# Local attention stage: norms ahead of the last rotation, long sums ahead of the outputs, some multiplies by broadcast sums later, and half of the turned queries copied on ScalarE

## The chip, the cores and the metric

The kernel runs on one core of a Trainium2 chip. The metric is device time in microseconds (us) of one execution. Engines are called as the profile does: PE is TensorE (PEld its weight loads), DVE is VectorE, ACT is ScalarE, POOL is GpSimd, and SP is SyncE, which issues nearly all DMAs here. Each engine works through its own instructions in order; between engines, semaphores order what depends on what.

## What is computed

The input x is (4, 512, 256) in fp32, with a small vector (4, 64) beside it. Three residual parts follow one another: a mixture of experts (the best 2 of 8) with a linear attention, a full attention with gates and 16 heads, and a local stage. The change lies in the last one. Its two layers, cut to what matters:

```python
for l in range(2):
    q, k, v = split(shift_token(y) @ wqkv[l])      # 8 heads of 64 each
    q, k = l2norm(q) * q_scale, l2norm(k) * k_scale
    q, k = rotary_xpos(q, k)                       # q * cos * s + rotate_half(q) * sin * s
    o = local_attention(q, k, v)                   # windows of 128: a key's own and the one before
    y = y + merge(o) @ wo[l]
    u, g = split(layernorm(shift_token(y)) @ w1[l] + b1[l])    # 256 -> 2 x 682
    y = y + (u * gelu(g)) @ w2[l] + b2[l]
out = y + x                                        # all in fp32
```

`shift_token` takes the second half of the channels from the token before. `l2norm` divides a head's vector by its norm.

## The kernel before, in words

The span falls into the two earlier parts (0 to 695 us) and the local stage, `local_stream` (L607 on, 695 to 1339 us), which goes through two layers with four batches each. A batch is 512 tokens, four tiles of 128 (`NT`). All of y stays on chip.

For each layer and batch:
- `front` (L634): y is transposed on PE (`pdt`) and projected (`pdq`). For each tile t and for s = 0 (queries) and 1 (keys), ACT squares the projection (L658), DVE sums the squares per head (`ss`, L659), DVE multiplies the projection, read from PSUM, by a table of cosines (`t1`, L661) and its two exchanged halves by one of sines (`t2`, L665, two instructions), and POOL adds both to `qr` (L668). After all eight, ACT takes the root of all norms (L672, for which ACT loads a table of functions), DVE bounds it (L673) and inverts it (L674). ACT copies the values (L680). DVE multiplies a tile's queries by 1/norm (L686); PE transposes queries and keys (`pqt`), DVE copies the turned queries to `qT` and ACT the turned keys to `kT` (L693). The keys' 1/norm goes into the exponential as its scale.
- `scores` (L702) for each of four head pairs c: scores on PE (`pds`), exponentials on ACT (L720), masks on DVE (L723 128x384, L726 128x64).
- `values` (L747): products with v (`pn`), put together from two banks by an ACT copy (L744) and a DVE addition (L745) into `oT`; POOL adds parts of p (L753), from which `sums` (L755), called for every second c, forms the softmax's sums: a product with ones (`pz`), `z` (L744, L745), then a chain on the SP queue: z to DRAM and back as 128 rows (`rden`, L768, L769), reciprocal on DVE (L770), out again (`rows`, L772) and back as a broadcast to 64 partitions each (`zb`, L775). DVE multiplies two tiles of oT by zb (L778).
- `tail` (L780): product with wo (`pdy`), added to y by DVE (L784).
- `normed` (L789): y's shifted half by three DMAs into `hn`, statistics (L800 to L802), root (L804, L805), normalization (L808). `turned` (L810): hn transposed (`pht`), `hT` on DVE (L817), and then POOL's long sums: y += fb2 over all four tiles (L821, 128x1024), in layer 1 also y += x (L824). `hidden` (L826): gates and values (`pug`, `pua`), GELU on ACT (L835), products on DVE (L836). `output` (L855): second product (`pfy`), added to y by DVE (L871), in layer 1 with the DMA to the output.

PE's order is written by hand: everything below `PE.in_order()` is pinned to program order on PE (`keep_in_program_order`). The main loop runs over steps k = 4b + c, and interleaves generators:

```python
for k in range(4 * B + 2):
    if k > 1 and k % 2:  sums(l, b0, ds[b0], c0)     # of step k - 2
    if 0 < k <= 4 * B:   values(ds[b0], c0)          # of step k - 1
    if b < B:            scores(ds[b], c)
    spend(6 if b < B - 1 else 3)                     # pieces of the next front, of tail, of the feed-forward
```

So a batch's front runs beside the attention of the batch before, and `tail` of batch b - 1 beside that of b. `feed_forward` (L877) of batch 0 to 2 begins beside the attention of the last batch, b = 3; there `turned` for batch b + 1 comes ahead of `output` for batch b. The order on the other engines is chosen by a scheduler with its own estimates, within what data and pinned instructions allow. PSUM has eight banks in one ring for all these products, so a late reader holds up PE.

Of the kernel before, what the change touches and what calls it, by code (L numbers as in the profile page):

```python
# [67 lines left out]
def adaln_attn_ffn_kernel(ctx: ExitStack, tc: tile.TileContext, a: dict, out: bass.AP):  # L68
# [44 lines left out]
    def mmt(name):  # L113
        return bank("mm", name)
# [492 lines left out]
    def local_stream(dw, lp, y, dr):  # L607
# [23 lines left out]
            load(w.w1, a["f_w1"][l].rearrange("(c p) o -> p c o", p=128))  # L631
            load(w.w2, a["f_w2"][l].rearrange("(c p) o -> p c o", p=128))

        def front(w, b, d):  # L634

            yT = lp.tile([128, 2, S + 1], F32, tag="yT", name="yT", bufs=1)
            nc.gpsimd.memset(yT[:, 1, 0:1], 0.0)
            for c in range(2):
                pt = mmt("pdt")
                for k in range(NT):  # L640
                    PE.transpose(pt[:, k * 128 : (k + 1) * 128], y[b][:, k, c * 128 : (c + 1) * 128], ident)
                nc.scalar.copy(yT[:, c, 1 : S + 1], pt)
                yield

            def project(t, s):
                lhs = [yT[:, 0, 1 + t * 128 : 1 + (t + 1) * 128], yT[:, 1, t * 128 : (t + 1) * 128]]
                ps = mmt("pdq")
                mm(ps, [(lhs[c], w.wqkv[:, c, s * DIN : (s + 1) * DIN]) for c in range(2)])
                return ps.rearrange("p (h d) -> p h d", d=DHD)

            d.ss = ss = lp.tile([128, NT, 2, DH], F32, tag="ss", name="ss")
            qr = []
            for t in range(NT):
                qr_t = lp.tile([128, 2, DH, DHD], F32, tag="qr", name="qr", bufs=4)
                for s in range(2):
                    p3 = project(t, s)
                    sq = lp.tile([128, DH, DHD], F32, tag="tmp", name="sq", bufs=3)
                    nc.scalar.activation(sq, p3, AF.Square)  # L658
                    nc.vector.reduce_sum(ss[:, t, s, :], sq, axis=AX.X)  # L659
                    t1 = lp.tile([128, DH, DHD], F32, tag="t1", name="t1")  # L660
                    nc.vector.tensor_tensor(  # L661
                        t1, p3, w.tab[:, 2 * s, t, :].unsqueeze(1).to_broadcast([128, DH, DHD]), ALU.mult)
                    t2 = lp.tile([128, DH, DHD], F32, tag="tmp", name="t2", bufs=3)
                    for d0, d1 in ((0, 32), (32, 0)):
                        nc.vector.tensor_tensor(  # L665
                            t2[:, :, d0 : d0 + 32], p3[:, :, d1 : d1 + 32],
                            w.tab[:, 2 * s + 1, t, d0 : d0 + 32].unsqueeze(1).to_broadcast([128, DH, 32]), ALU.mult)
                    nc.gpsimd.tensor_tensor(qr_t[:, s], t1, t2, ALU.add)  # L668
                    yield
                qr.append(qr_t)  # L670

            nc.scalar.activation(ss, ss, AF.Sqrt)  # L672
            nc.vector.tensor_scalar_max(ss, ss, 1e-12)  # L673
            nc.vector.reciprocal(ss, ss)  # L674
            d.v = lp.tile([128, NT, DH, DHD], F32, tag="v", name="v")
            d.kT = lp.tile([128, 4, S], F32, tag="kT", name="kT")
            d.qT = lp.tile([128, 4, S], F32, tag="qT", name="qT")

            def value(t):
                nc.scalar.copy(d.v[:, t], project(t, 2))  # L680

            for t in range(3):
                value(t)
                yield
            for t in range(NT):
                nc.vector.tensor_tensor(  # L686
                    qr[t][:, 0], qr[t][:, 0], ss[:, t, 0].unsqueeze(2).to_broadcast([128, DH, DHD]), ALU.mult)
                for s, dst in enumerate((d.qT, d.kT)):
                    pt = mmt("pqt")
                    for c in range(4):  # L690
                        PE.transpose(pt[:, c * 128 : (c + 1) * 128],
                                     qr[t][:, s, 2 * c : 2 * c + 2, :].rearrange("p h d -> p (h d)"), ident)
                    (nc.vector.tensor_copy if s == 0 else nc.scalar.copy)(  # L693
                        dst[:, :, t * 128 : (t + 1) * 128], pt.rearrange("p (c q) -> p c q", q=128))
                    yield
                if t == 1:
                    value(3)
                    yield
# [53 lines left out]
                p = d.ps[c, r].rearrange("p (j q) -> p j q", q=192)  # L752
                nc.gpsimd.tensor_tensor(p[:, 1:, 0:64], p[:, 1:, 0:64], p[:, : NT - 1, 128:], ALU.add)  # L753

        def sums(l, b, d, c):  # L755
            z = lp.tile([128, S], F32, tag="z", name="z", bufs=1)
            pz = [mmt("pz") for g in range(2)]
            for i in range(4):
                ii = slice(32 * i, 32 * i + 32)
                p = d.ps[c - 1 + i // 2, i % 2].rearrange("p (j q) -> p j q", q=192)  # L760
                later = pz[1][ii].rearrange("p (j q) -> p j q", q=128)
                PE.matmul(pz[0][ii], ones32[0:64], p[0:64, :, 0:128], start=True, stop=True)
                PE.matmul(later[:, :, 64:], ones32[64:], p[64:, :, 0:64], start=True, stop=True)
                PE.matmul(later[:, 1:, 0:64], ones32[64:], p[64:, : NT - 1, 64:128], start=True, stop=True)
            together(z, pz)
            rd = rdenl[:, (l * B + b) * 2 + c // 2, :]
            sums_ = dr.tile([4, S], F32, tag="sums", name="sums")
            nc.sync.dma_start(sums_, z[0:128:32, :])  # L768
            nc.sync.dma_start(rd, sums_.rearrange("h q -> (h q)").rearrange("(p n) -> p n", p=128))  # L769
            nc.vector.reciprocal(rd, rd)  # L770
            rows_ = dr.tile([4, S], F32, tag="rows", name="rows")
            nc.sync.dma_start(rows_.rearrange("h q -> (h q)").rearrange("(p n) -> p n", p=128), rd)  # L772
            zb = lp.tile([128, 2, S], F32, tag="zb", name="zb", bufs=1)
            for r in range(2):
                nc.sync.dma_start(zb[64 * r : 64 * r + 64],  # L775
                                  rows_.rearrange("(c r) q -> r c q", r=2)[r].partition_broadcast(64))
            for i in range(2):
                nc.vector.tensor_tensor(d.oT[c - 1 + i], d.oT[c - 1 + i], zb[:, i, :], ALU.mult)  # L778

        def tail(w, b, d):  # L780
            for t in range(NT):
# [29 lines left out]
        def turned(l, b, f):  # L811
            f.hT = lp.tile([128, 2, S], F32, tag="hT", name="hT")
            for c in range(2):
                pt = mmt("pht")
                for k in range(NT):
                    PE.transpose(pt[:, k * 128 : (k + 1) * 128], f.hn[:, k, c * 128 : (c + 1) * 128], ident)
                nc.vector.tensor_scalar(f.hT[:, c, :], pt, col("lg", 2 * l + c), col("lb", 2 * l + c),  # L817
                                        ALU.mult, ALU.add)
                yield

            nc.gpsimd.tensor_tensor(  # L821
                y[b], y[b], row("fb2")[:, l * H : (l + 1) * H].unsqueeze(1).to_broadcast([128, NT, H]), ALU.add)
            if l == 1:
                nc.gpsimd.tensor_tensor(y[b], y[b], xres[b], ALU.add)  # L824

        def hidden(l, w, f):  # L826

# [49 lines left out]
        def feed_forward(l, w):  # L877
            fs = [SimpleNamespace() for b in range(B)]
            normed(0, fs[0])
            yield  # L880
            yield from turned(l, 0, fs[0])
            for b in range(B):
                for i, _ in enumerate(hidden(l, w, fs[b])):
                    yield b
                    if i == 0 and b + 1 < B:
                        normed(b + 1, fs[b + 1])
                if b + 1 < B:
                    yield from turned(l, b + 1, fs[b + 1])
                yield from output(l, w, b, fs[b])


# [7 lines left out]

        def first_two(w, ds):
            first, second = (front(w, b, ds[b]) for b in range(2))

            def lead():
                for _ in range(20):
# [5 lines left out]
                yield from first  # L912
            return lead(), [second] + [front(w, b, ds[b]) for b in range(2, B)]

        lead, second = first_two(wa, ds)
        run(lead)
        with PE.in_order():
            for l in range(2):
# [26 lines left out]
                def spend(n):  # L945
                    for _ in range(n):
                        next(fill, None)

                for k in range(4 * B + 2):
                    b, c = divmod(k, 4)  # L950
                    if k > 1 and k % 2:
                        b0, c0 = divmod(k - 2, 4)
                        sums(l, b0, ds[b0], c0)
                    if c == 0 and b < B:
                        run(fill)
                        fill = beside(b)
                    if 0 < k <= 4 * B:
                        b0, c0 = divmod(k - 1, 4)
                        values(ds[b0], c0)
                    if b < B:  # L960
                        scores(ds[b], c)
                    spend(6 if b < B - 1 else 3)
# [21 lines left out]
                nxt = iter(())  # L984
                if l == 0:
                    wa = attn_weights(1)
                    nxt, second = first_two(wa, ds)
                for at in ff:
                    if at is not None and at >= 2:
                        break  # L990
# [1124 lines left out]
```

## Time and profile before

| | |
|---|---|
| runs, us | 1336.31, 1340.78, 1344.16 |
| median, us | 1340.78 |
| profiled execution, us | 1341.16 |
| its span, us | 1339.4 |
| mean granted clock of PE | 0.983 |
| POOL busy, us | 292.8 (22%) |
| DMA, mean over the span | 64 GB/s |

The span is the stretch from the first to the last instruction of the profiled execution; its own time is 1.8 us longer. In timeline lines of the profile the first two numbers are the start and the duration in us, then come engine, line, operation, output<-input by the program's names, shape, and in brackets the idle time of the engine before it with what ended that; "x2" stands for two like instructions in a row, and the duration is then of both. A line of waits gives the waiting group, what released it, the sum, the number of times and the longest. The granted clock is the share of PE's full clock that it was allowed.

### The profile page before, as it was taken

Reading aid. Unit: us, or ns where it says so; the run is one execution under the profiler, and the core shown is the slowest. Engines: PE = TensorE matmul, PEld = TensorE weight load, DVE = VectorE, ACT = ScalarE, POOL = GpSimd, SP = SyncE. Lnnn points to the kernel's source line nnn. Section 1 sums busy time; section 2 is a strip of 40 time slices with the busy share of each in tenths; the row PEclk is TensorE's granted clock in tenths of the full one; section 3 lists DMA queues with packets and bytes.
Section 4 is the critical chain, followed back from the end, with each engine's and each line's share of the span. In section 5 each row is a group of like instructions: output and inputs, shape, how many; then the busy total and the mean of one; then the engine's idle time right before and its main releaser. Section 6 shows DMA issues by size and latency. Waiting matters only on the chain.

```text
span 1339.4 us, 23071 instructions
## 1 busy us (share of the span) xinstructions
PE 1273.7 (95%) x9214; PEld 812.9 (61%) x9214; DVE 685.6 (51%) x1464; ACT 581.6 (43%) x1158; POOL 292.8 (22%) x321
## 2 busy tenths in 40 slices
PE   4899999998999999999999999999999998999998
PEld 3788899964566634444344655766556556667654
DVE  6221243425777734241247798654362877864421
ACT  3221233226655365656644646561222655464111
POOL 1322356420000201010103334210030333422010
PEclk7999999998999999999999999999999999999999
DMA  3565666523000000000220001311001011012000
GB/s 95 212 232 199 233 235 226 183 101 101 0 1 1 1 1 1 0 1 1 91 71 1 18 18 27 104 34 25 24 0 44 25 30 31 18 43 57 17 20 23
DMA packets 41856, 85.29 MB, mean 64 GB/s; under 512 B 9409, under 2 KB 25673, under 8 KB 39433
## 3 DMA queue, kind: packets, MB, share of 16 engines
q1 hardware_dynamic: 36600, 73.02, 16.9%
q0 software_dynamic: 3504, 9.46, 2.1%
q8 instruction: 77, 1.26, 0.4%
q10 hardware_dynamic: 1632, 1.21, 0.3%
q14 instruction: 43, 0.34, 0.1%
HBM read 74.76 MB, written 6.82 MB: 61 GB/s over the span
## 4 chain that ended last, share of the span: by engine, by line
PE 76%; DVE 10%; DMA 6%; ACT 4%; issue 3%; POOL 0%; SPq 0%; DVEq 0%; POOLq 0%
PE ph L82 11%; PE pdq L82 7%; PE pfy L82 6%; PE sc L82 6%; PE pua L82 5%; PE pug L82 5%; PE pv L82 5%; PE pdy L82 4%; PE po L82 3%; PE pn L82 3%; DMA ys<-ob,goal 2%; PE pds L82 2%; PE pqk L82 2%; PE pz L82 1%; PE pqt L86 1%
## 5 line engine op out<-in xcount | busy, mean ns | idle before, releaser
L82 PE MATMUL pdq<-wqkv,yT 128*128 128x512 f32 x384 | 172.4, 599 | 2.5 <-DVE t L665 2.2
L424 ACT ACTIVATE cex<-sc 128x512 f32<-128x512 f32 x256 | 132.0, 605 | 85.8 <-PE sc L82 84.8
L82 PEld LDWEIGHTS pdq<-wqkv,yT 128*128 128x128 f32 x384 | 71.5, 191 | 85.0 <-issue 76.7
L82 PE MATMUL ph<-h,w 128*128 128x256 f32 (+2 forms) x576 | 121.4, 369 | 0.3 <-ACT h L1635 0.3
L668 POOL TENSOR_TENSOR qr<-t,t 128x512 f32<-128x512 f32 x64 | 81.3, 1271 | 138.2 <-DVE t L665 138.2
L82 PEld LDWEIGHTS ph<-h,w 128*128 128x128 f32 x576 | 101.5, 191 | 15.7 <-ACT h L1635 0.5
L1500 DVE TENSOR_SCALAR h<-ph,w 128x256 f32<-128x256 f32 (+2 forms) x52 | 23.0, 462 | 122.1 <-PE ph L82 101.6
L82 PE MATMUL sc<-qm,kT 32*128 32x512 f32 x512 | 83.0, 647 | 0.0
L720 ACT ACTIVATE p<-pds,ss 128x192 f32<-128x192 f32 (+1 forms) x256 | 79.8, 425 | 2.1 <-PE pds L82 0.8
L82 PE MATMUL pua<-hT,w 128*128 128x512 f32 x160 | 75.3, 593 | 1.1 <-DVE z L745 1.1
L82 PE MATMUL pug<-hT,w 128*128 128x512 f32 x160 | 76.1, 598 | 0.0
L658 ACT ACTIVATE sq<-pdq 128x512 f32<-128x512 f32 x64 | 38.5, 601 | 84.0 <-POOL qr L668 46.6
L753 POOL TENSOR_TENSOR p<-p 128x192 f32<-128x192 f32 x64 | 42.1, 678 | 137.7 <-PE pn L82 134.9
L835 ACT ACTIVATE gl<-pug,cols 128x512 f32<-128x512 f32 x40 | 27.3, 687 | 93.3 <-PE pug L82 90.4
L82 PE MATMUL pv<-cex,v 128*32 128x512 f32 x512 | 61.7, 598 | 2.7 <-DVE vw L378 2.7
L82 PE MATMUL pfy<-w,uA 128*128 128x256 f32 x256 | 61.4, 383 | 0.0
L82 PE MATMUL po<-w,h 128*128 128x256 f32 x264 | 60.1, 380 | 0.0
L723 DVE TENSOR_TENSOR p<-p,lmask 128x384 f32<-128x384 f32 x64 | 47.1, 736 | 23.2 <-ACT p L720 21.8
L82 PE MATMUL pdy<-wo,oT 128*128 128x256 f32 x256 | 58.7, 383 | 0.0
L1498 ACT ACTIVATE h<-ph,w 128x256 f32<-128x256 f32 (+2 forms) x52 | 22.4, 455 | 82.5 <-PE ph L82 78.7
L82 PE MATMUL pn<-p,v 64*64 64x128 f32 (+1 forms) x1792 | 50.4, 254 | 7.6 <-DVE p L726 3.7
L836 DVE SCALAR_TENSOR_TENSOR uA<-pua,cols,gl 128x512 f32<-128x512 f32 x32 | 23.8, 749 | 65.6 <-PE pua L82 56.1
(361 smaller groups left out, 2325.1 us busy)
## 6 DMA issues: line engine op xcount, KB each, us to landing
w<-in_moe_w_dram SPq DMA_DIRECT2D x18, 1024.0 KB, 8.3
w<-in_moe_w_dram SPq DMA_DIRECT2D x18, 516.0 KB, 3.8
w<-in_moe_w_dram SPq DMA_DIRECT2D x14, 640.0 KB, 4.3
zb<-rows SPq DMA_DIRECT2D x32, 256.0 KB, 4.2
g<-ys SPq DMA_DIRECT2D x6, 512.0 KB, 6.4
wqkv<-in_f_wqkv_dram SPq DMA_DIRECT2D x2, 1536.0 KB
w<-in_f_w_dram SPq DMA_DIRECT2D x2, 1408.0 KB
w<-in_moe_w_dram SPq DMA_DIRECT2D x4, 512.0 KB
```

The lines of the kernel that those rows point to most:

```text
L82: cls._queue(nc.tensor.matmul(*args, **kw))
L86: cls._queue(nc.tensor.transpose(*args, **kw))
L424: nc.scalar.activation(ex[:, i, :], pss[2 * j + i], AF.Exp, scale=CHD**-0.5)
L658: nc.scalar.activation(sq, p3, AF.Square)
L668: nc.gpsimd.tensor_tensor(qr_t[:, s], t1, t2, ALU.add)
L720: nc.scalar.activation(p[:, j * 192 : j * 192 + n], pss[j // 2][r][:, j % 2 * 192 : j % 2 * 192 + n], AF.Exp, scale=d.ss[:, j, 1, 2 * c + ...
L723: nc.vector.tensor_tensor(edges, edges, lmask[:, :128].rearrange("p (s q) -> p s q", q=64).unsqueeze(1).to_broadcast([128, 3, 2, 64]), ALU ...
L753: nc.gpsimd.tensor_tensor(p[:, 1:, 0:64], p[:, 1:, 0:64], p[:, : NT - 1, 128:], ALU.add)
L835: nc.scalar.activation(gl, pg, AF.Gelu, bias=col("bg", l * (NU + 1) + i))
L836: nc.vector.scalar_tensor_tensor(f.u[i // 4][:, i % 4, :], pa, col("ba", l * (NU + 1) + i), gl, ALU.add, ALU.mult)
L1498: pinned(nc.scalar.activation(dst, src, AF.Relu, bias=bias))
L1500: pinned(nc.vector.tensor_scalar(dst, src, bias, 0.0, ALU.add, ALU.max))
```

## The change

- In `front`, the root, the bound and the reciprocal stand after t1 of the last projection (t = 3, s = 1) and ahead of its t2, and so do the multiplies by 1/norm of the query tiles 0 and 1. DVE's instructions among these, and the last two halves of t2, are pinned to program order. Tiles 2 and 3 are multiplied where they were.
- In the very first front (`awake=4`), ACT takes a root of one element early, and PE makes four products of 128x128 into the bank of the first `pqt` ahead of its transposes.
- The turned queries of the tiles 1 and 3 are copied by ACT.
- POOL's long sums leave `turned(l, b)` for a new `residual(l, b)`, pinned, ahead of `output(l, b)`.
- The multiplies by zb become a function that `sums` returns. For c0 = 1 it is called one step later, after `values`, and pinned; for batch 2 and c0 = 3 two steps later, inside the next `sums` behind z, and pinned; for the others at once, as before.

PE's order is the same but for the four products, SP's is the same. In the built kernel the multiplies by zb stand elsewhere on DVE at three steps: for batch 1, c0 = 1, they come after the two additions of `oT` at k = 8; for batch 2, c0 = 3, after z at k = 15; for batch 3, c0 = 1, after the two additions of `oT` at k = 16. The sums of batch 0 and 1 on POOL stand right after the last additions of p (k = 16), with a clearing of `hn` behind each. Those of batch 2 and 3 stand, in layer 0, after the fifth and the eighth addition of `qr` of the next layer's first front, and in layer 1 after the last clearing of `hn`.

```diff
-        def front(w, b, d):
+        def front(w, b, d, awake=0):
...
             qr = []
+            if awake:
+                root = lp.tile([128, 1], F32, tag="rs", name="root")
+                nc.scalar.activation(root, eps5, AF.Sqrt)
+
+            def unit(t):
+                tc.keep_in_program_order(nc.vector.tensor_tensor(
+                    qr[t][:, 0], qr[t][:, 0], ss[:, t, 0].unsqueeze(2).to_broadcast([128, DH, DHD]), ALU.mult))
+
             for t in range(NT):
...
                         t1, p3, w.tab[:, 2 * s, t, :].unsqueeze(1).to_broadcast([128, DH, DHD]), ALU.mult)
+                    if t == NT - 1 and s == 1:
+                        nc.scalar.activation(ss, ss, AF.Sqrt)
+                        tc.keep_in_program_order(nc.vector.tensor_scalar_max(ss, ss, 1e-12))
+                        tc.keep_in_program_order(nc.vector.reciprocal(ss, ss))
+                        for t0 in range(2):
+                            unit(t0)
                     t2 = lp.tile([128, DH, DHD], F32, tag="tmp", name="t2", bufs=3)
                     for d0, d1 in ((0, 32), (32, 0)):
-                        nc.vector.tensor_tensor(
+                        ins = nc.vector.tensor_tensor(
                             t2[:, :, d0 : d0 + 32], p3[:, :, d1 : d1 + 32],
                             w.tab[:, 2 * s + 1, t, d0 : d0 + 32].unsqueeze(1).to_broadcast([128, DH, 32]), ALU.mult)
+                        if t == NT - 1 and s == 1:
+                            tc.keep_in_program_order(ins)
                     nc.gpsimd.tensor_tensor(qr_t[:, s], t1, t2, ALU.add)
...
-            nc.scalar.activation(ss, ss, AF.Sqrt)
-            nc.vector.tensor_scalar_max(ss, ss, 1e-12)
-            nc.vector.reciprocal(ss, ss)
             d.v = lp.tile([128, NT, DH, DHD], F32, tag="v", name="v")
...
             for t in range(NT):
-                nc.vector.tensor_tensor(
-                    qr[t][:, 0], qr[t][:, 0], ss[:, t, 0].unsqueeze(2).to_broadcast([128, DH, DHD]), ALU.mult)
+                if t > 1:
+                    nc.vector.tensor_tensor(
+                        qr[t][:, 0], qr[t][:, 0], ss[:, t, 0].unsqueeze(2).to_broadcast([128, DH, DHD]), ALU.mult)
                 for s, dst in enumerate((d.qT, d.kT)):
                     pt = mmt("pqt")
+                    if t + s == 0 and awake:
+                        with PE.in_order():
+                            for _ in range(awake):
+                                PE.matmul(pt[:, 0:128], ident, ident, start=True, stop=True)
                     for c in range(4):
...
                                      qr[t][:, s, 2 * c : 2 * c + 2, :].rearrange("p h d -> p (h d)"), ident)
-                    (nc.vector.tensor_copy if s == 0 else nc.scalar.copy)(
+                    (nc.vector.tensor_copy if s == 0 and t % 2 == 0 else nc.scalar.copy)(
                         dst[:, :, t * 128 : (t + 1) * 128], pt.rearrange("p (c q) -> p c q", q=128))
...
-        def sums(l, b, d, c):
+        def sums(l, b, d, c, before):
             z = lp.tile([128, S], F32, tag="z", name="z", bufs=1)
...
             together(z, pz)
+            if before is not None:
+                before(True)
             rd = rdenl[:, (l * B + b) * 2 + c // 2, :]
...
                                   rows_.rearrange("(c r) q -> r c q", r=2)[r].partition_broadcast(64))
-            for i in range(2):
-                nc.vector.tensor_tensor(d.oT[c - 1 + i], d.oT[c - 1 + i], zb[:, i, :], ALU.mult)
+
+            def scaled(pin):
+                for i in range(2):
+                    ins = nc.vector.tensor_tensor(d.oT[c - 1 + i], d.oT[c - 1 + i], zb[:, i, :], ALU.mult)
+                    if pin:
+                        tc.keep_in_program_order(ins)
+            return scaled
...
-            nc.gpsimd.tensor_tensor(
-                y[b], y[b], row("fb2")[:, l * H : (l + 1) * H].unsqueeze(1).to_broadcast([128, NT, H]), ALU.add)
+        def residual(l, b):
+            tc.keep_in_program_order(nc.gpsimd.tensor_tensor(
+                y[b], y[b], row("fb2")[:, l * H : (l + 1) * H].unsqueeze(1).to_broadcast([128, NT, H]), ALU.add))
             if l == 1:
-                nc.gpsimd.tensor_tensor(y[b], y[b], xres[b], ALU.add)
+                tc.keep_in_program_order(nc.gpsimd.tensor_tensor(y[b], y[b], xres[b], ALU.add))
...
                     yield from turned(l, b + 1, fs[b + 1])
+                residual(l, b)
                 yield from output(l, w, b, fs[b])
...
-        def first_two(w, ds):
-            first, second = (front(w, b, ds[b]) for b in range(2))
+        def first_two(w, ds, awake):
+            first, second = front(w, 0, ds[0], awake), front(w, 1, ds[1])
...
-        lead, second = first_two(wa, ds)
+        lead, second = first_two(wa, ds, 4)
         run(lead)
...
+                late = {}
                 for k in range(4 * B + 2):
...
                         b0, c0 = divmod(k - 2, 4)
-                        sums(l, b0, ds[b0], c0)
+                        scaled = sums(l, b0, ds[b0], c0, late.pop(k, None))
+                        due = k + (1 if c0 == 1 else 2 if b0 == B - 2 else 0)
+                        if due == k:
+                            scaled(False)
+                        else:
+                            late[due] = scaled
                     if c == 0 and b < B:
...
                         values(ds[b0], c0)
+                    if k in late:
+                        late.pop(k)(True)
                     if b < B:
...
                     wa = attn_weights(1)
-                    nxt, second = first_two(wa, ds)
+                    nxt, second = first_two(wa, ds, 0)
                 for at in ff:
...
                         break
```

## The prediction

> **What bounds the kernel now.** I read the page from the top: busy time, the slices, then the chain that ended last.
>
> ```profile
> PE 1273.7 (95%) x9214; PEld 812.9 (61%) x9214; DVE 685.6 (51%) x1464; ACT 581.6 (43%) x1158; POOL 292.8 (22%) x321
> ...
> PE 76%; DVE 10%; DMA 6%; ACT 4%; issue 3%; POOL 0%; SPq 0%; DVEq 0%; POOLq 0%
> ```
>
> TensorE (PE) is busy for 95% of the span. The change leaves its work alone (but for four 128x128 matmuls), so only PE's idle time and its clock can be won. Second come PE's waits in the local stage (690 to 1340 us), as releaser, sum, times, longest:
>
> ```profile
> PE pqt L86 <- DVE qr L686: 9.5, 7, 2.5
> PE pn L82 <- DVE p L726: 3.7, 2, 2.3
> PE pn L82 <- DVE p L723: 3.6, 4, 0.9
> PE pdq L82 <- DVE t L665: 2.2, 4, 0.7
> PE pds L82 <- DVE t L665: 2.2, 3, 1.0
> PE pua L82 <- DVE z L745: 1.1, 1, 1.1
> ```
>
> The reader sees that all of this is 23 us, and that VectorE (DVE) releases nearly all of it. Third, stretches of one clock step around two of the three largest gaps (PE, PEld, DVE, ACT, POOL busy, granted clock, DMA share, GB/s):
>
> ```profile
> 714.56:717.97 3.41, 0.89 (x8) 0.82 (x8) 2.74 (x5) 1.03 (x3) 1.11 (x1) 1.00 0.00 0
> 717.97:721.38 3.41, 3.41 (x13) 2.60 (x12) 2.16 (x4) 1.17 (x2) 0.00 (x0) 0.50 0.00 0
> 1127.57:1130.98 3.41, 1.06 (x30) 0.68 (x28) 3.41 (x3) 1.99 (x5) 3.19 (x3) 1.00 0.63 154
> 1130.98:1134.39 3.41, 3.41 (x62) 3.23 (x62) 3.24 (x5) 1.33 (x4) 1.74 (x2) 0.50 0.01 2
> ```
>
> After a stretch with over 2.3 us of idle PE the clock is 0.50 for 3.41 us, and so it is after the third, 1182.18 to 1185.59, with 2.38 idle. That costs half of it, 1.7 us, on top of the gap. The dips' starts lie whole multiples of 3.413 us apart (121 from the first to the second), so whether a gap near 2.3 us brings one depends on where it falls; I take one half.
>
> Last, the DVE's order around the gap at 1127.71, and POOL beside it:
>
> ```profile
> 1126.42 2.19 DVE L723 TENSOR_TENSOR p<-p,lmask 128x384 f32<-128x384 f32 x1 [0.45 <-ACT p L720]
> 1128.53 2.36 DVE L726 TENSOR_TENSOR p<-p,lmask 128x64 f32<-128x64 f32 x1
> ```
>
> ```profile
> 1125.19 3.00 POOL L821 TENSOR_TENSOR yc<-yc,drows 128x1024 f32<-128x1024 f32 x1 [3.49 <-DVE hn L808]
> 1128.13 0.10 POOL L637 MEMSET yT<- 128x1 f32 x1
> 1128.27 2.54 POOL L824 TENSOR_TENSOR yc<-yc,xres 128x1024 f32<-128x1024 f32 x1
> ```
>
> Undisturbed, the two masks take 0.56 and 0.22 us; beside a long sum they end with it. Instructions of DVE that read PSUM (0.68 and 0.41 us for L661 and L665) do not grow beside POOL. So two inputs from SBUF on DVE and a sum on POOL exclude each other, one whole instruction at a time. Beside this, the Trainium skill ("SBUF — State Buffer", section "Who interferes with whom") calls the pair's shared port an exclusive lock; the masks agree, and by it the moved multiplies of part F, for which there is no row, would be held just like them.
>
> **The change part by part**, against the profiled execution (1341.16 us, span 1339.4; the median of the runs is 1340.78). Negative is a gain.
>
> A, first front. PE waits 2.52 us at 714.66 for the unit queries (L686).
>
> ```profile
> 713.58 0.75 DVE L665 TENSOR_TENSOR t<-pdq,tab 128x256 f32<-128x256 f32 x2
> 715.16 0.56 DVE L673 TENSOR_SCALAR ss<-ss 128x64 f32<-128x64 f32 x1 [0.84 <-ACT ss L672]
> 715.76 0.55 DVE L674 RECIPROCAL ss<-ss 128x64 f32<-128x64 f32 x1
> 716.35 1.89 DVE L686 TENSOR_TENSOR qr<-qr,ss 128x512 f32<-128x512 f32 x3
> ```
>
> With the table loaded ahead (1.28 us) and two t2 halves (0.75) out of the way, the Sqrt runs at 713.6 behind a v copy of ACT, maximum 0.18, reciprocal 0.55 and the first multiply 0.68 end at 715.3, not 717.0: 1.7 us off the gap. What is left is about 0.75 us, so the dip goes too, 1.7 us. Late next is ACT, which gets two query copies (0.58 each, as its copies of kT) ahead of the exponentials: these start about 724.25 and not 727.07. **-2.8** (-1.1 if there had been no dip).
>
> The four matmuls stand in what is left of the gap, and cost nothing while it is over 1 us; else up to 4 x 0.16 us (a pqt transpose: 0.63 for four). Beside it, the Trainium skill ("TensorE: Matmul & The Clock Gate", "Part 1: The HAM clock gate") halves the clock after a wholly idle window of some 3.4 us; the window agrees with the 3.413 us here, but not the idle share, since 2.35 of 3.41 was enough. By that rule none of these gaps would bring a dip, and the change would be worth 3.4 us less.
>
> B, fronts of b=1, no sums near (749.05, 1.04 us; 1062.76, 1.04). The first multiply no longer stands behind the last halves (0.75) nor beside the last qr addition (0.5): PE 1.0 earlier, of which the next z keeps 0.25. **-0.75 twice**. In layer 1 the query copy of t=3 goes ahead of the first exponentials: 0.58 by its row, 0.27 after the slack there. **+0.3**.
>
> C, fronts of b=2 with sums in the masks. Layer 0: gaps 791.03 (1.14) and 813.06 (0.94) go. PE gains 1.9, but in the next stretch DVE is the later one (its reductions stand behind a multiply by zb that waits until 816.61 for its DMA): **-1.4** stays. Layer 1: 0.95 + 1.40 (the sums in the masks), 1.1 of the multiply gap 1105.65 (1.15) and the dip's 1.7 would make 5.15; the sums' removal leaves exponentials as next late, so **-4.4** (-3.5 for another place on the clock's steps).
>
> D, fronts of b=3 (840.19, 1.12; 1157.78, 1.52). DVE must now wait for the Sqrt, which has a v copy and a table load (1.28) ahead of it: 0.5 to 1.2 us of idle DVE with the last halves, a value copy and the multiply by zb queued behind it. **-0.9** and **-1.25**. The cover is thin: pdy needs oT at 844.95 and I find the multiply's end at 844.75.
>
> E, the multiplies said to be later. In the built order those before 870.91 and 1182.74 keep their place; z at 1172.94 to zb at 1183.05 is a chain of DMAs on SP that is not shortened. The gaps (1.10 and 2.27) stay. The dip at the second is a coin toss, -0.9 in the mean.
>
> F, long sums before outputs, b=3. This speaks against the change. For batches 0 and 1 the sums come to stand right behind POOL's last p additions, which end at 902.91, with nothing to wait for. Just there DVE gets its multiplies by zb:
>
> ```profile
> 903.56 1.29 DVE L778 TENSOR_TENSOR oT<-oT,zb 128x512 f32<-128x512 f32 x2 [2.53 <-DMA zb<-rows]
> 904.77 1.15 DVE L745 TENSOR_TENSOR oT<-pn,oT 128x448 f32<-128x448 f32 x2
> ...
> 907.80 0.61 DVE L745 TENSOR_TENSOR z<-pz,z 128x448 f32<-128x448 f32 x1
> ...
> 918.96 1.29 DVE L778 TENSOR_TENSOR oT<-oT,zb 128x512 f32<-128x512 f32 x2 [2.45 <-DMA zb<-rows]
> ```
>
> The two oT rows now come ahead of the multiplies. Sum 0 runs 902.95 to 905.33 (2.38, its row at 914.02), the first multiply to 905.9, sum 1 to 908.3, the second multiply to 908.9. Then y, two hT, statistics and z follow as in the trace: z ends 2.85 later than 908.41. From z to the last zb are 10.5 us of DMAs and a reciprocal behind statistics that slip too, so zb lands at 921.9, not 918.96; with the multiply (0.65) oT is ready at 922.55, where PE wants it for pdy at 920.2, and 0.25 goes for the fourth part of oT. **+2.6**. Layer 1 has two sums a batch: z 2.5 later, zb at 1241.85, oT at 1242.5, wanted at 1240.76, and 0.15 in the same way: **+1.9**. Bounds: 0 if the second multiply gets in between the sums (z then fits its slack of 0.55 and 0.83); +1.7 more if the first gap halves the clock, +0.85 in the mean.
>
> G. Sums 2 and 3 of layer 0 stand among the next layer's qr additions (1.27 each), where PE has no gaps: 0; if that cover fails, one sum, 2.4. Sixteen copies leave DVE (0.69 each) for ACT (0.58), 44% busy: 0 outside A and B.
>
> Sum: -2.8 - 0.75 - 1.4 - 0.9 + 2.6 + 0.3 - 0.75 - 4.4 - 1.25 + 1.9 = -7.45; the two mean dips (-0.9, +0.85) cancel. 1341.16 - 7.45 = 1333.7, **1334 us**.
>
> **The rivals.**
> R1, no collision in F: the second multiply gets in first. For: memsets stand between the sums. Against: a multiply already held while a sum runs, as the masks above. -7.45 - 4.5: 1329.
> R2, slower: the pinned queue on DVE decides. In six inner fronts the maximum waits up to 1.2 us for the Sqrt, and a held instruction 1.27 (a qr addition); halves and multiplies by zb queue behind, and PSUM's banks with them. It decides once the multiply by zb is later than pdy (0.2 us of slack, D). 6 x 2.47 = +14.8: 1348.5. For: D's thin slack. Against: at 748.06 the maximum follows without a wait.
> R3, no difference: the table loads and copies on ACT become the late ones in A and C, so -2.8, -1.4 and half of -4.4 go: 1340.
> R4, the dips stay, since other gaps bring them: -7.45 + 3.4: 1337. This is also what the page's rule on idle windows would give; three dips behind three largest gaps speak against it.
>
> **How the numbers follow.** Forecast 0.47 (own range 1331 to 1337), R1 0.20, R2 0.12, R3 0.13, R4 0.08. The range reaches from R1 with an end of its own (E's dip, 1.7) to R3 with the bounds of F and A: 1327 to 1343.5; R2 and thin tails stay out. A change under 0.5% (6.7 us, below 1334.1) cannot be told from none here: half of the forecast and all of R1 are faster, 0.44; the rest, R3 and R4 same, 0.44; R2 slower, 0.12.
>
> **What would show it.** A: pqt starts near 715.4 and no 0.50 clock follows. B, D: waits of pqt for L686 fall from 9.5 to about 3 us. C: masks of b=2 at 0.56 and 0.22. E: the gap at 1182.74 is still there. F: multiplies L778 near 903 stretched to over 1.5 us, and pdy waiting near 920. It is wrong if those stay 0.65 each, or if DVE idles for L672 while PE waits for pdy.

## The result and the profile after

The median goes from 1339.54 us (21 runs, 1335.57 to 1346.53) to 1335.37 us (21 runs, 1330.7 to 1339.1). The ratio is 0.9963, with a 95% interval of 0.9952 to 0.9975: 3 to 6 us faster. The forecast was 1334, from a sum of -7.45 us. The profiled executions differ by 5.9 us (1341.16 and 1335.27; spans 1339.4 and 1333.5), the medians by 4.2. The forecast subtracted its sum from the one profiled execution, which lies 1.6 us above the median of the 21; so the time of 1334 was met more closely (1.4 us) than the gain.

PE's waits in the local stage after (releaser, sum, times, longest). Lines have moved: L679 is t2, L658 the early unit multiply, L800 the multiply by zb, L741 and L744 the masks, L763 the additions into oT and z:

```profile
PE pdy L82 <- DVE oT L800: 4.0, 2, 2.4
PE pdq L82 <- DVE t L679: 3.2, 4, 0.9
PE pua L82 <- DVE z L763: 2.7, 1, 2.7
PE pn L82 <- DVE p L744: 2.2, 1, 2.2
PE pds L82 <- DVE t L679: 1.8, 3, 1.0
PE pn L82 <- DVE p L741: 1.7, 2, 0.8
PE pqt L86 <- DVE qr L658: 1.5, 4, 0.4
```

The first line of before, pqt for the unit queries with 9.5 us, is now the last with 1.5. A line that before did not have, pdy for oT with 4.0 us, heads the list. One wait has been exchanged for another.

To see where the time went, I took the start of the same PE instructions in both traces and followed their difference through the stage. Each step of it belongs to one part of the prediction:

| part, at (before's time) | forecast | measured |
|---|---|---|
| A, first front (717 to 722) | -2.8 | -3.5 |
| B, layer 0 (750) | -0.75 | -0.7 |
| C, layer 0 (792 to 831) | -1.4 | -1.4 |
| D, layer 0 (841) | -0.9 | -0.7 |
| E, layer 0 (871) | 0 | +1.65 |
| F, layer 0 (921) | +2.6 | +2.0 |
| B, layer 1 (1064 to 1070) | -0.45 | -0.5 |
| C, layer 1 (1107 to 1149) | -4.4 | -4.5 |
| D, layer 1 (1159) | -1.25 | -1.1 |
| E, layer 1 (1188) | 0 (mean of a dip -0.9) | -1.7 |
| F, layer 1 (1241) | +1.9 | +4.5 |

With +0.15 ahead of the stage and -0.2 of rests the measured column gives the -5.9, but for rounding. The two misses in E nearly cancel; both are luck, as is worked out below.

Stretches of one clock step after, with the columns as before (PE, PEld, DVE, ACT, POOL busy, granted clock, DMA share, GB/s). The first is the stretch that had 2.52 us of idle PE; the others lie around the second wait of pdy, in layer 1:

```profile
714.56:717.97 3.41, 3.41 (x27) 3.02 (x26) 3.38 (x7) 1.94 (x4) 1.20 (x1) 1.00 0.00 0
1230.12:1233.53 3.41, 1.03 (x5) 0.33 (x4) 1.35 (x3) 0.00 (x0) 0.00 (x0) 1.00 0.42 121
1233.53:1236.94 3.41, 3.41 (x6) 1.85 (x6) 1.32 (x3) 0.00 (x0) 0.00 (x0) 0.50 0.00 0
```

So the first front has neither gap nor half clock any more, and the new gap of 2.38 us has brought one. That is 1.7 of the 4.5 us of F in layer 1.

VectorE and POOL at the place of part F, layer 0, after:

```profile
898.39 1.16 DVE L763 TENSOR_TENSOR oT<-pn,oT 128x448 f32<-128x448 f32 x2 [1.86 <-ACT oT L762]
899.47 4.59 DVE L800 TENSOR_TENSOR oT<-oT,zb 128x512 f32<-128x512 f32 x2
903.98 0.41 DVE L809 TENSOR_TENSOR yc<-pdy,yc 128x256 f32<-128x256 f32 x1
```

```profile
898.37 2.37 POOL L847 TENSOR_TENSOR yc<-yc,drows 128x1024 f32<-128x1024 f32 x1
900.67 0.20 POOL L818 MEMSET hn<- 1x128 f32 x1
900.84 2.67 POOL L847 TENSOR_TENSOR yc<-yc,drows 128x1024 f32<-128x1024 f32 x1
```

The two multiplies took 1.29 us before and take 4.59 now: the first ends half a microsecond after sum 0 (900.74), the second after sum 1 (903.51). The masks of batch 2, layer 1, are undisturbed in return:

```profile
1121.50 0.55 DVE L741 TENSOR_TENSOR p<-p,lmask 128x384 f32<-128x384 f32 x1
1121.97 0.22 DVE L744 TENSOR_TENSOR p<-p,lmask 128x64 f32<-128x64 f32 x1
1122.64 0.56 DVE L741 TENSOR_TENSOR p<-p,lmask 128x384 f32<-128x384 f32 x1 [0.46 <-ACT p L738]
```

### The profile page after: what moved, and what is told of

Read it like the earlier page. It is cut to its first block, busy times and chain, and to the rows that moved or that the text cites. A ratio compares the mean times of both kernels' runs of the same rounds, so it can differ in the third digit from the quotient of the medians.

```text
span 1333.5 us, 23089 instructions
## 1 busy us (share of the span) xinstructions
PE 1273.4 (95%) x9222; PEld 809.9 (61%) x9222; DVE 672.4 (50%) x1448; ACT 588.7 (44%) x1175; POOL 294.6 (22%) x321
## 3 DMA queue, kind: packets, MB, share of 16 engines
q10 hardware_dynamic: 1632, 1.21, 0.3%
## 4 chain that ended last, share of the span: by engine, by line
PE 72%; DVE 9%; DMA 9%; ACT 6%; issue 3%; POOL 1%; SPq 0%; POOLq 0%; DVEq 0%
PE ph L82 11%; PE pdq L82 7%; PE sc L82 6%; PE pv L82 5%; PE pug L82 5%; PE pua L82 5%; PE pfy L82 5%; PE pdy L82 4%; PE po L82 3%; PE pn L82 3%; DMA zb<-rows 2%; DMA ys<-ob,goal 2%; PE pqk L82 2%; PE pds L82 1%; PE pf L82 1%
## 5 line engine op out<-in xcount | busy, mean ns | idle before, releaser
L82 PEld LDWEIGHTS pdy<-wo,oT 128*128 128x128 f32 x256 | 47.9, 191 | 16.2 <-DVE oT L800 5.7
L82 PEld LDWEIGHTS pua<-hT,w 128*128 128x128 f32 x160 | 30.3, 190 | 41.5 <-issue 35.8
```

What stands on the lines that cost most here:

```text
L82: cls._queue(nc.tensor.matmul(*args, **kw))
```

## The experiments

The theory was that the norms' move is the gain, and that moving the sums gives back in F about what it wins in C. The rival was that the sums' move is itself the gain and pdy's new wait comes from something else. Ratios are to the kernel before, run on the same chip. The changed kernel's own ratio is 0.9963 [0.9952, 0.9975].

**Hold the sums behind the multiplies.**

```diff
         def residual(l, b):
+            if b < 2:
+                gate = lp.tile([1, 1], F32, tag="gate", name="gate", bufs=1)
+                tc.keep_in_program_order(nc.gpsimd.tensor_copy(
+                    gate, y[0][0:1, 0, 0:1] if b else ds[B - 1].oT[1][0:1, 0:1]))
```

> The changed kernel, with the long sums of batches 0 and 1 held back by a copy of one element: for batch 0 it reads oT of the last batch behind its multiplies by zb, for batch 1 it reads y of batch 0 behind its outputs. The order on every other engine is that of the changed kernel. Theory (the sums exclude the multiplies, and what follows on VectorE is late for pdy): the pair of multiplies takes 1.3 us and not 4.59, the two waits of pdy (1.61 and 2.38 us) and the half clock behind the second (1.7 us) go, and the time falls by 4 to 5 us, to about 1330.5. Rival (the broadcast itself lands late, by its DMAs or because the multiplies stand behind the two additions of oT): the pair is short, but pdy still waits over 1.5 us twice and the time is that of the changed kernel within 1 us.

Measured: 1335.36 us, ratio 0.9969 [0.9955, 0.9983]. Neither theory had this right. VectorE in layer 1 of this run, and POOL beside it:

```profile
1213.58 1.29 DVE L800 TENSOR_TENSOR oT<-oT,zb 128x512 f32<-128x512 f32 x2
...
1221.23 2.12 DVE L833 TENSOR_SCALAR hn<-yc,mv,rs 128x128 f32<-128x128 f32 x1
1223.28 2.49 DVE L833 TENSOR_SCALAR hn<-hn,mv,rs 128x128 f32<-128x128 f32 x1
1225.69 0.24 DVE L790 RECIPROCAL rden<-rden 128x16 f32<-128x16 f32 x1
```

```profile
1215.07 2.35 POOL L851 TENSOR_TENSOR yc<-yc,drows 128x1024 f32<-128x1024 f32 x1
1217.49 2.35 POOL L854 TENSOR_TENSOR yc<-yc,xres 128x1024 f32<-128x1024 f32 x1
1220.79 0.17 POOL L849 COPY gate<-yc 1x1 f32<-1x1 f32 x1 [0.95 <-DVE yc L901]
1220.93 2.34 POOL L851 TENSOR_TENSOR yc<-yc,drows 128x1024 f32<-128x1024 f32 x1
1223.35 2.34 POOL L854 TENSOR_TENSOR yc<-yc,xres 128x1024 f32<-128x1024 f32 x1
```

The multiplies are short, as the theory said. But sum 1 now meets the normalization, and two of its instructions go from 0.34 to 2.12 and 2.49 us. The reciprocal of the softmax's sums stands right behind them, so the broadcast is late again and pdy waits 3.15 us. What I had missed is that an instruction with only one large input can be held as well. Sum 0, from 1215.07 to 1219.84, held nothing.

**Undo the sums' move.**

```diff
+            nc.gpsimd.tensor_tensor(
+                y[b], y[b], row("fb2")[:, l * H : (l + 1) * H].unsqueeze(1).to_broadcast([128, NT, H]), ALU.add)
+            if l == 1:
+                nc.gpsimd.tensor_tensor(y[b], y[b], xres[b], ALU.add)
...
-                residual(l, b)
                 yield from output(l, w, b, fs[b])
```

> The changed kernel with one part undone: POOL's long sums stand in turned again, not pinned. The order of PE, VectorE, ScalarE and SP is that of the changed kernel. Theory (moving the sums took stalls from the masks and gave others to the multiplies, of about the same size): the masks of batch 2 are stretched to over 2 us again (PE waits of 0.9, and of 0.9 and 1.4 us, for them), pdy no longer waits, and the time is within 1.5 us of the changed kernel's. Rival 1 (the sums' move is where the gain came from): slower by 3 us or more, back at the kernel before. Rival 2 (the stalls of the multiplies cost more than those of the masks): faster by 2 us or more.

Measured: 1331.28 us, ratio 0.9934 [0.9915, 0.9954]; the median is 4.1 us below the changed kernel's, and the intervals just touch. That is rival 2. The masks are stretched again:

```profile
1117.76 2.72 DVE L741 TENSOR_TENSOR p<-p,lmask 128x384 f32<-128x384 f32 x1
1120.40 2.36 DVE L744 TENSOR_TENSOR p<-p,lmask 128x64 f32<-128x64 f32 x1
```

For them PE waits 0.78 us in layer 0, and 0.78 and 2.26 us with a half clock behind it in layer 1, but pdy does not wait at all. The sums' move as made is a loss.

**Undo the norms' move** (root, bound and reciprocal behind the rotations, unit multiplies in the loop of the transposes, nothing pinned there).

> The changed kernel with one part undone: root, bound and reciprocal behind all rotations, and all four unit multiplies where the kernel before has them; the early table load and the four products stay. Theory (the wait of the first pqt for the first unit multiply is what the norms' move removes): six waits of about 1.0 to 1.5 us return at the inner fronts, of which 4.5 to 5.5 us stay in the time, and some 0.8 us at the first front: slower by 5 to 6 us. Rival (VectorE waits for the root in the moved order, so the queue behind it costs what the move gains): within 1.5 us of the changed kernel.

Measured: 1341.86 us, ratio 1.0018 [1.0006, 1.0030], 6.5 us above the changed kernel. PE's first waits:

```profile
PE pqt L86 <- DVE qr L695: 7.2, 7, 1.2
PE pdy L82 <- DVE oT L795: 4.3, 2, 2.2
```

All six inner waits are back, at 1.04 to 1.21 us. The norms' move is the whole gain of the change and more.

**VectorE copies all turned queries.**

```diff
-                    (nc.vector.tensor_copy if s == 0 and t % 2 == 0 else nc.scalar.copy)(
+                    (nc.vector.tensor_copy if s == 0 else nc.scalar.copy)(
```

> The changed kernel with one part undone: VectorE copies all turned queries again. Theory (ScalarE's sixteen copies delay the exponentials at the first front by 0.6 us and twice by 0.3, and VectorE has room for its copies in the inner fronts): the same within 1 us, rather faster. Rival 1 (VectorE is what holds the stretches behind the fronts of batches 1 to 3, so each copy that returns costs there): slower by 2 us or more. Rival 2 (ScalarE is what holds them): faster by 2 us or more.

Measured: 1333.51 us, ratio 0.9948 [0.9928, 0.9967], which overlaps the changed kernel's. By medians it is 1.9 us faster, near the edge of rival 2, but the two profiles, which differ by 0.6 us in all, have a step of 2.2 us at one broadcast near 863, of which more below.

**Only sum 0 ahead of its output.** The gate of the first experiment for b = 0, and the sums of batches 1 to 3 back in `turned`, still pinned.

> The changed kernel, but of the long sums only that of batch 0 stands ahead of its output, held back by a copy of one element of oT behind the multiplies by zb; those of batches 1 to 3 stand in turned again. Orders of the other engines as in the changed kernel. The run with the sums held back had shown that a sum which falls beside the normalization (L808 of the kernel before) stretches it from 0.34 to over 2 us, so that the rival there was right in time for another reason. Theory (every instruction of VectorE that reads only SBUF through two streams or in its fast form is held by a sum, and the place decides): sum 0 at 899 and 1215 to 1220 lies beside additions from PSUM only, the others lie behind the normalizations; no stretched masks at b = 2, no stretched multiplies, the waits of pdy under 0.3 us: 6 to 8 us faster than the changed kernel, 1327 to 1329.5. Rival (pdy waits for the broadcast's DMAs anyway): 1331 to 1333, as with all sums back in turned.

Measured: 1330.58 us, ratio 0.9946 [0.9924, 0.9967], between the two. In layer 0 pdy waits no more. In layer 1 it does (1.95 us): the pinned sum of batch 1 again stands behind the last additions of p, and the multiplies take 4.57 us.

**Also put off the multiplies of batch 2, c0 = 1, by two steps.**

```diff
-                        due = k + (1 if c0 == 1 else 2 if b0 == B - 2 else 0)
+                        due = k + (2 if b0 == B - 2 else 1 if c0 == 1 else 0)
```

> As the run before, and also the multiplies of batch 2, c0 = 1, put off by two steps, into the next sums behind z, pinned (the changed kernel asks for one step, and the built order leaves them where they were). Theory (these multiplies wait for their broadcast's DMAs, and z in layer 0 and the masks in layer 1 wait behind them): the waits of pua for z (0.5 to 2.7 us in the profiles so far) and of pn for the masks near 1175 (2.0 to 3.3 us, and mostly the half clock behind it) go: 3 to 5 us less than the run before. Rival (the multiplies are then late for the sums of c0 = 3, whose broadcast shares the one zb buffer, or for pdy of batch 2): the waits reappear as pdy for oT, within 1.5 us of the run before.

Measured: 1325.46 us, ratio 0.9903 [0.9885, 0.9921]. The waits of pua for z and of pn for L744 are gone, and nothing takes their place: 5.1 us, a little over what the theory gave. VectorE's multiplies and POOL in layer 1 show what is left:

```profile
1205.36 4.57 DVE L800 TENSOR_TENSOR oT<-oT,zb 128x512 f32<-128x512 f32 x2
```

```profile
1204.26 2.36 POOL L852 TENSOR_TENSOR yc<-yc,drows 128x1024 f32<-128x1024 f32 x1
1206.70 2.68 POOL L855 TENSOR_TENSOR yc<-yc,xres 128x1024 f32<-128x1024 f32 x1
```

**The same, with VectorE's copies.**

> As the run before, and VectorE copies all turned queries, as in the kernel before. Theory (the copies on ScalarE put off exponentials, VectorE's copies lie in cover): 1 to 2 us less than the run before, as the same edit gave on the changed kernel (1333.5 against 1335.4, whose intervals overlap). Rival (that difference was noise of the broadcast's landing, 2.3 us of it at one wait near 863): the same within 0.7 us.

Measured: 1326.5 us, ratio 0.9912 [0.9894, 0.9930]. That is 1.0 us above the run before by the medians, with intervals that overlap widely: the theory's gain is not there, and the rival's 0.7 us is finer than six executions can tell. Who copies the queries makes no difference that these runs show.

**All multiplies by zb at once, as before** (`due = k`, on the changed kernel).

> The changed kernel with one part undone: all multiplies by zb at once, not pinned, as in the kernel before. They then stand ahead of the additions of oT at k = 8 and k = 16 and among the products of the feed-forward before k = 15. Theory (the moved multiplies had no wait to remove, since the two with waits keep their place): within 1 us of the changed kernel. Rival (standing ahead of the additions, the multiplies of the last batch escape the sums, or the additions escape the DMA's wait): faster or slower by over 1.5 us.

Measured: 1333.72 us, ratio 0.9968 [0.9955, 0.9981]: 1.7 us below the changed kernel by the medians, 0.7 above it by the ratios, so no difference is shown. The profile, of the slowest of the twelve executions, has a wait that the changed kernel has not:

```profile
PE pfy L82 <- DVE oT L763: 2.7, 2, 1.3
```

Standing ahead of the additions of oT, the held multiplies delay these, and PE waits for them once in each layer; its waits of pdy are shorter in return (1.17 and 1.94 us, for 1.61 and 2.38). Putting these multiplies off as the change does exchanges one wait for part of another, and is worth nothing that the times show.

**Sums in turned not pinned.** As the version with one sum and late multiplies, but without `keep_in_program_order` around the sums of batches 1 to 3.

> As the run with one sum and the multiplies put off by two steps, but the long sums in turned not pinned (they still stood pinned in that run, and in layer 1 that of batch 1 came to stand behind the last additions of p again: multiplies of 4.57 us at 1205 and a wait of pdy of 2.27). The other engines' orders stay. Theory (this collision alone is what is left of part F): sum 1 of layer 1 runs near 1180 as in the kernel with all sums back in turned, multiplies 1.29, no wait of pdy over 0.3 us, no half clock behind it: 2 to 4 us less, 1321.5 to 1323.5. Rival (pdy waits for the broadcast's DMAs, which are issued at the same time in any order): within 1 us of 1325.5.

Measured: 1324.53 us, ratio 0.9890 [0.9874, 0.9907]. (Five of its six executions took 1321.8 to 1326.1 us; the sixth is spoken of below.) By time it is only 0.9 us below the version before it, or 1.4 if the long execution is left out, less than the theory's 2 to 4. By its profile the theory holds; PE's longest waits are

```profile
PE pdq L82 <- DVE t L679: 3.2, 4, 0.9
PE pds L82 <- DVE t L679: 1.9, 3, 1.0
PE pn L82 <- DVE p L741: 1.7, 2, 1.0
PE pqt L86 <- DVE qr L658: 1.4, 3, 0.5
```

There is no wait of pdy, no gap over 1 us, and no half clock in the stage until its last microseconds; the gaps sum to 9.7 us, against 23.4 before.

**Without the four products in the first front** (`range(0)` in place of `range(awake)`, on that version).

> As the run before it in this list, without the four products of 128x128 ahead of the first pqt (the early table load stays). Theory (in the changed kernel's profile they fill 714.66 to 715.71, and the first transposes start 0.2 us behind the unit queries; what they would prevent is a half clock, which has so far followed no gap under 1.9 us): a gap of about 0.7 us is back, no half clock behind it, time the same within 0.7 us, rather 0.2 less. Rival (a gap there brings the clock down in half of the executions): slower by 0.9 us or more.

Measured: 1324.33 us, ratio 0.9888 [0.9871, 0.9905]. The gap of 0.75 us is there, no half clock follows it, and the time is the same. The products do nothing.

**Only the two steps of the multiplies, on the changed kernel.**

> The changed kernel with the multiplies of batch 2, c0 = 1, put off by two steps, as in the runs above, and nothing else. Theory (part E is a gain of its own, which the change missed by placing these multiplies one step later, where the broadcast has not landed): waits of pua for z and of pn for the masks of L744 near 1175 go, those of pdy stay: 3 to 5 us faster than the changed kernel, 1330.5 to 1332.5. Rival (without the sums' mending the time won ahead is lost at pdy, which waits for the broadcast of c0 = 3): under 1.5 us.

Measured: 1329.33 us, ratio 0.9940 [0.9923, 0.9957]; 6.0 us by the medians, 3 by the ratios. pdy still waits (2.4 and 2.2 us), the other two waits are gone. The gain is its own.

**The best version once more.**

> The same kernel as in the run with the sums in turned not pinned, once more: five of its six executions took 1321.8 to 1326.1 us, one took 2139.82, which is longer by 815 us, about what the second pass through the later stages takes that the kernel holds ready for sums whose reciprocals are out of bounds. Theory (a rare event that has nothing to do with where sums and multiplies stand): all executions between 1320 and 1328, median 1324 to 1325. Rival (the new order brings it about): again one or more executions near 2140.

Measured: 1322.97 us, ratio 0.9895 [0.9878, 0.9911], all four executions between 1321.8 and 1325.66. The long one did not come again; one event among ten executions leaves its cause open. None of the 99 executions of the changed kernel and the other versions took more than 1343.54 us, so the order of this version is not cleared. That the long execution was the second pass is inferred from its length alone, since no trace of it was kept.

## Why the prediction was right, and where its sum was off

**A was right.** The chain of root, bound, reciprocal and multiply ends 1.7 us earlier, the half clock goes, and the first exponentials start at 723.94, not 727.07. Nothing of the rival with ScalarE's copies (1340 us) showed: taking them back changed the time by -1.9 us on the changed kernel and by +1.0 us in the seventh run, neither of which can be told from nothing.

**B, C and D were right to within 0.3 us each.** The removal of the norms' move shows that they are the norms' doing (7.2 us of waits come back, all but 0.4 of them at the inner fronts), and the removal of the sums' move shows the same for the masks in C. The rival of a queue behind the norms on VectorE (1348.5 us) is refuted by the same runs: with the moved norms no wait of pqt in an inner front is longer than 0.51 us in any profile.

**E was wrong in layer 0.** I took the wait behind the broadcast as fixed. SP's issues in before and after, and the multiply that waits for them:

```profile
858.94 0.39 SPq L199 DMA_DIRECT2D wqkv<-in_f_wqkv_dram  x1
859.93 1.26 SPq L775 DMA_DIRECT2D zb<-rows  x2
...
869.02 1.29 DVE L778 TENSOR_TENSOR oT<-oT,zb 128x512 f32<-128x512 f32 x2 [2.25 <-DMA zb<-rows]
```

```profile
852.99 0.39 SPq L199 DMA_DIRECT2D wqkv<-in_f_wqkv_dram  x1
853.98 1.26 SPq L795 DMA_DIRECT2D zb<-rows  x2
...
864.52 1.29 DVE L800 TENSOR_TENSOR oT<-oT,zb 128x512 f32<-128x512 f32 x2 [3.89 <-DMA zb<-rows]
```

The 1536 KB of the next layer's wqkv are issued 1 us ahead of this broadcast. From its issue to the multiply it took 9.1 us before and 10.5 us after, and 8.7 to 10.4 in the twelve other profiles, against 5.1 for the first broadcast of layer 0, at 765.1. The same broadcast of layer 1, where no weights are loaded ahead of it, took 5.0 us before and 5.1 after. So +1.65 is mostly the luck of one transfer, and not an effect of the change. That the transfer holds the broadcast up I infer from this order and these times; a run with wqkv loaded later was not made. What follows from it was tested: with the multiply out of the way of z, pua waits no more. In layer 1 the gap stayed as forecast (2.19 us for 2.27), but no half clock followed it as one had before, which is the -1.7: luck too, the other way.

**F was right in its mechanism, and 2 us too small.** The multiplies are held by the sums as worked out; layer 0 came to 2.0 for 2.6. In layer 1 the gap was 2.38 for 1.9, because from the end of z (1221.18) to the multiply (1232.18) it took 11.0 us, where the forecast had 10.25, and the half clock fell behind this gap, where I had put its mean of 0.85 behind the other.

```profile
1220.57 0.61 DVE L763 TENSOR_TENSOR z<-pz,z 128x448 f32<-128x448 f32 x1
...
1232.18 1.29 DVE L800 TENSOR_TENSOR oT<-oT,zb 128x512 f32<-128x512 f32 x2 [4.63 <-DMA zb<-rows]
```

The first experiment then showed the rule to be wider than I had used it: the normalization, one input of 128x128 and two scalars a partition, is held too (0.34 to 2.18, 2.12 and 2.49 us). Additions that read PSUM, the statistics and hT from PSUM were not (beside the sums of layer 1 after, z took 0.61 us, a statistic 0.28 and two hT 1.51, within 0.02 of what they took in the kernel before without a sum). Beside this, the Trainium skill ("SBUF — State Buffer", section "Who interferes with whom") says that copies and tensor_scalar can run in a mode that takes both of VectorE's ports, the shared one with them, if their operands allow it; these rows agree, and hT, the same operation from PSUM, fits as well.

**Where the gain went.** By medians the norms give 6.5 us and the sums' move takes 4.1 of them back; copies, products and the multiplies as moved give nothing that could be measured. Of the -4.2 us this leaves -1.8, which fits the early table load of A but was not run alone. The trace without the norms' move shows it in its place: behind the first front PE is still 2.8 us ahead of the kernel before, of the 3.5 in the changed kernel, and no half clock falls there; what is left of A in it are the early load, the copies and the four products, and the last two gave nothing when taken out of other versions. The forecast had let C and F come out nearly even (-5.8 with the norms' share, +4.5); measured by taking it out, the sums' move loses. What decides is the place that `residual` gives the sums: in layer 1 the sum of batch 1 ran at 1204.26 in the version with it pinned and at 1178.57 with it not pinned. Behind the last additions of p, where no data keep them longer, the sums meet multiplies that z stands behind, and from z a chain of DMAs leads to pdy.

**The half clock.** Counting all fourteen profiles of the stage, 15 of the 23 gaps of 1.9 to 3.4 us were followed by it (two that a few matmuls split are counted whole), and none under 1.9 (the drain at the end of the kernel aside). It lasted 3.41 us thirteen times and 6.83 us twice. The forecast's one half was, if anything, somewhat low. The Trainium skill ("TensorE: Matmul & The Clock Gate", "Part 1: The HAM clock gate") has the clock at half after at least one idle window of some 3.4 us. The length agrees with the 3.41 us here, the idle window does not: in the one before the first half clock PE was busy for 0.89 of its 3.41 us.

## What to carry to other kernels

Before a long GpSimd instruction is moved, list for its new place which VectorE instructions read only SBUF (two tensors, or one in a scaling), and which of them a DMA chain or TensorE waits for; move it beside instructions that read PSUM. A part that removes a stall has to be run alone: here one part gave all and another took most of it back, and the sum of both looked like a small success. A multiply that waits for a transfer belongs behind the work that does not need it; for those of batch 2 one step was too early here, two were right.

## What was not expected

- The scaling of one 128x128 tile on VectorE took 0.34 us alone and 2.1 to 2.5 us beside a 128x1024 sum on GpSimd.
- Four products of 128x128 in fp32 took 1.05 us (eight records in the trace), not the 0.63 us of four transposes from which I had priced them.
- A broadcast issued 1 us behind a load of 1536 KB on the same queue took 8.7 to 10.5 us to its use; the others that a multiply waited for took 4.6 to 6.1.
